# A planned kernel of two graph layers: columns for the attention vectors, reliefs by rows, last stores by halves of rows, and another plan

## The chip, the cores and the metric

The kernel runs on one core of a Trainium2 chip. A core has TensorE (PE: matmuls, each with a load of weights, PEld), VectorE (DVE), ScalarE (ACT), GpSimd (POOL) and SyncE (SP, which here only issues DMAs). Each engine takes its own instructions in order; engines wait for each other by semaphores. The metric is the time of one execution on the device in microseconds (us). Everything is float32.

## The reference

64 graphs of 256 nodes with 256 features, with an adjacency matrix of small integers each, go through two layers. Cut to what matters:

```python
def gat(h, adj, W, a):                       # layer 0, twice: (W1, a1), then (W2, a2)
    Wh = h @ W
    e = leaky_relu(Wh @ a[:256] + swap(Wh @ a[256:]), 0.2)
    att = softmax(where(adj > 0, e, -9e15), axis=1)
    return att @ Wh
h = layernorm(x + gat(gat(x, adj, W1, a1), adj, W2, a2))
x = layernorm(h + relu(h @ w_ff1 + b_ff1) @ w_ff2 + b_ff2)

q, k = x @ Wq + bq, x @ Wk + bk              # layer 1, 8 heads of 32
attn = softmax(q k^T / sqrt(32))
o = sum over r of (attn * (adj == r)) @ (x @ Wv[r] + bv[r])
x = layernorm(x + o @ Wo + bo)
x = layernorm(x + gelu(x @ W1 + b1) @ W2 + b2)
```

## The kernel before

The kernel works on 32 pairs of graphs. One pair goes through `whole_way` (line 1212): `gat_layers` (639), `feed_forward` (stage 0), `attention`, `feed_forward` (stage 2), and two stores (line 1222, 256 KB each). All of a pair's rows lie in a tile `x` of 128 partitions and four blocks of 256 columns: block 2b+j holds the rows 128j to 128j+127 of graph b.

**Matmuls.** A product is written as four strips of 32 weight columns (`by_strips`, line 164), so nearly every matmul of a pair has line 164; in this trace each float32 matmul leaves two records. The products of the feed-forwards and of queries, keys and values are done by a scheme of seven products of blocks in the place of eight: class `Blocks` has the steps `p1` to `p7` (16 records each), with sums of blocks made on DVE before and after; a feed-forward runs two such sets, called a and b, and its second product is `by_seven` (line 887), seven products of 64 records. Attention computes `scores` for a group of four heads, exponentials on ACT (line 1041), mask and half sums on DVE (1045, 1049), then `products` (1063, 1066), `invert` and divide (1075 to 1086), and at the end `into_rows` for each of the two graphs. Four such groups make a pair.

**Layouts.** Rows become columns by a way through DRAM: DVE turns blocks of 32 (line 773), SP stores them (`home`, 778) and gathers them (`yT`, 784, four DMAs). Where that is too slow, at the first and last pairs (`hurried`), PE transposes (`transposed_on_tensor`, line 804).

**The plan.** Which instruction comes next on which engine is decided when the program is built, by a list scheduler in the kernel itself (`run`, line 286). Each pair is a generator; what it yields is a step for PE with the events that it needs, a name that it must hold alone, and buffers. Work for the other engines is handed over by `put` with an assumed cost, a rank and an assumed delay. `run` always takes the earliest thing that can start; among several it goes by `DEGREE` (for PE) or by `RANK` (for the others). `FIRST`, `QKV` and `GROUPS` give the order of the seven products and of the heads, `FLIGHT` the number of pairs under way, `SLACK` how long a step must have been ready, and `CHANGES` (line 32) replaces any of these at given times of the plan's own clock. The resulting order is fixed: the engines take it as it is, however long things last. `START`, `LANDED` and `THERE` (lines 67 to 69) are assumed times at which engines begin and first DMAs land.

**The opening.** Line 173 loads W2 by SP's queue; ACT's queue loads W1 transposed, then a2, broadcast to all partitions (256 KB written), then a1 as columns (2 KB). DVE multiplies W2's rows with a2 and sums them (line 179, four times), which gives the columns W2 a2 beside W2. PE then multiplies W1 with all of it, 256 wide columns and 4 narrow ones per half of W1's rows, and DVE and ACT copy the result to `w12` (lines 188, 189), the weights of the first layer's matmul on xT. Behind these, SP issues every other first load, 13.8 MB in the first 45 us.

**Reliefs.** Layer norm biases and output biases are added to rows once; what they would add wrongly to later products is taken from those products' biases. `relieve` (line 1171) does this for both feed-forwards and for queries and keys: for each block of 128 columns of a weight matrix it makes that block the stationary operand and the bias one moving column, which gives the correction along the partitions:

```python
nc.tensor.matmul(p[:, m:m + 1], lhsT=w[:, ((0, 1), (2, 6))[half][c], rows + at * P:rows + (at + 1) * P],
                 rhs=more[1][:, c:c + 1], start=c == 0, stop=c == KC - 1)
```

One DVE subtraction (line 1181) follows. `relieve_values` does the same for values by rows, with the bias broadcast as stationary operand. `block_sums` and `last_sums` then make the sums of weights that the seven products need.

**Layer norm.** `layernorm` (line 717): ACT squares with a sum (726), POOL takes the root (731, 732), DVE centres and scales (737, 740), each for two blocks of rows. Ahead of it the mean comes either from DVE's addition of rows (`add_rows`, 698) or, after `by_seven`, from ACT (`means`, 712). It takes the blocks of one graph, 2b and 2b+1.

Of the kernel before, what the change touches and what calls it, by code (L numbers as in the profile page):

```python
# [10 lines left out]
F32 = mybir.dt.float32  # L11
# [3 lines left out]
AF = mybir.ActivationFunctionType  # L15
# [15 lines left out]
NORMED = ()  # L31
CHANGES = (
    (27.0, ("rank", "centre", 2),
     ("all", "first", ("a1", "b1", "a2", "a6", "b2", "b6", "a5", "a7", "b7", "b5", "a4", "b4", "a3"))),
    (117.0, ("rank", "piece", 3), ("rank", "halves", -1)),
    (207.0, ("all", "slack", 0.4), ("rank", "exp", -2), ("rank", "scale", 2)),
    (297.0, ("degree", "gat", -1)),
    (387.0, ("degree", "first", -1)),
    (477.0, ("rank", "halves", 2), ("rank", "v", -0.5)),
    (567.0, ("all", "slack", 0.1)),  # L40
    (657.0, ("all", "first", ("a1", "b1", "b2", "a2", "a6", "b6", "a5", "a7", "b7", "b5", "a4", "b4", "a3"))),
    (747.0, ("all", "slack", 0.6), ("rank", "act", -1), ("rank", "turn", 0), ("rank", "divide", 0), ("degree", "fill", 1.5),
     ("rank", "qk", 2)),
    (837.0, ("rank", "mask", -0.5), ("rank", "centre", 2)),
    (927.0, ("rank", "addends", 2)),
    (1017.0, ("rank", "means", -2), ("rank", "sums", -2), ("all", "slack", 0.4)),
    (1197.0, ("rank", "mask", 1)),
    (2187.0, ("rank", "mask", -0.5)),
    (2277.0, ("rank", "exp", -0.5), ("rank", "halves", -0.5)),
    (2457.0, ("rank", "squares", 3)),  # L50
    (2547.0, ("all", "slack", 0.3)),
    (2637.0, ("rank", "normalise", 1.5), ("degree", "first", 2)),
    (2727.0, ("rank", "centre", 1), ("rank", "turn", 1), ("all", "slack", 0)),
    (2817.0, ("all", "slack", 0.2), ("rank", "means", 3)),
# [6 lines left out]
        "normalise": -1, "copies": -2, "seeds": -2, "act": -1, "last": -1, "sums": -0.5, "qk": 1, "v": 1.5, "exp": 3, "mask": 0, "halves": 0, "invert": 3,  # L61
# [5 lines left out]
START = {"tensor": 9.5, "vector": 9.3, "scalar": 9.7, "gpsimd": 0.0, "sync": 36.0}  # L67
LANDED = (("ln0", 15.0), ("ff0", 18.5), ("ff0_last", 26.0), ("ln1", 28.5), ("attention", 34.5), ("ff1", 40.0), ("ff1_last", 43.0))
THERE = ((6.5, 8.0, 13.5), (9.5, 11.0, 27.5), (20.5, 22.0, 35.0))
# [3 lines left out]
def two_layers(ctx: ExitStack, tc: tile.TileContext, t: dict, out: bass.AP, flag: bass.AP):  # L73
# [22 lines left out]
    PART = 64  # L96
# [74 lines left out]
    a2, w1T = passing[:, 0], passing[:, 1].rearrange("p (c m) -> p c m", c=KC)  # L171
    junk = work.tile([P, 2, N], F32, name="h", bufs=HQ)[:, 0]
    nc.sync.dma_start(right[:, :, :D], t["L0_gnn_W2"].rearrange("(c p) m -> p c m", p=P))
    nc.scalar.dma_start(w1T, t["L0_gnn_W1T"].rearrange("(c p) m -> p c m", p=P))
    nc.scalar.dma_start(a2, bass.AP(tensor=t["L0_gnn_a2"].tensor, offset=t["L0_gnn_a2"].offset, ap=[[0, P], [1, 2 * D]]))
    nc.scalar.dma_start(right[:, :, D + 2:], t["L0_gnn_a1c"])
    for s in range(2):
        for c in range(KC):
            nc.vector.scalar_tensor_tensor(
                junk, right[:, c, :D], 1.0, a2[:, s * D:(s + 1) * D], op0=ALU.mult, op1=ALU.mult,  # L180
                accum_out=right[:, c, D + s:D + s + 1])
    both = [bank() for _ in range(KC)]
    for m in range(KC):
        for columns in (slice(0, D), slice(D, D + 4)):
            for c in range(KC):
                by_strips(both[m][:, columns], lhsT=w1T[:, c, m * P:(m + 1) * P], rhs=right[:, c, columns],
                          start=c == 0 and columns.start == 0, stop=c == KC - 1, skip_group_check=True)
    nc.vector.tensor_copy(w12[:, 0], both[0][:, :D + 4])
    nc.scalar.activation(w12[:, 1], both[1][:, :D + 4], AF.Copy)

# [163 lines left out]
    def done_with(name):  # L358
        del alone[name]

# [276 lines left out]
    def gat_layers(pair, to, loads):  # L637
# [37 lines left out]
        for b in range(2):  # L675
# [9 lines left out]
            transposed(to["x"], layernorm(to["x"], ln[0], b, added, biased[0], stage="gat"), normal, b, pair, 0)  # L685
# [19 lines left out]
    def means(y, b, *events):  # L705

        of = {}

        def mean(j):
            if j == 0:  # L710
                of["less"] = small.tile([P, 2], F32, name="less", bufs=8)
            nc.scalar.activation(unread, y[:, 2 * b + j, :], AF.Copy, scale=-1.0 / D, accum_out=of["less"][:, j:j + 1])

        return of, put_each("scalar", 0.45, [lambda j=j: mean(j) for j in range(2)], *events, rank=rank_of["means"])

    def layernorm(r, gb, b, added, *events, stage=None):
# [3 lines left out]
        rows = [r[:, 2 * b + j, :] for j in range(2)]  # L720
# [7 lines left out]
        def root():  # L728
# [4 lines left out]
            if stage in NORMED:  # L733
                nc.gpsimd.tensor_tensor(of["less"], of["less"], rstd, ALU.mult)
# [7 lines left out]
        def normalise(j):  # L742
            nc.scalar.activation(rows[j], rows[j], AF.Identity, bias=of["less"][:, j:j + 1], scale=rstd[:, j:j + 1])

        def onto_all(n, op):
            both = r[:, of_graph(b), :]
            nc.vector.tensor_tensor(both, both, gb[n].rearrange("p (k d) -> p k d", k=1).to_broadcast([P, 2, D]), op)
# [940 lines left out]
```

## Time and profile before

| | us |
|---|---|
| median of 3 runs | 2898.7 |
| lowest and highest | 2896.8, 2900.65 |
| the profiled execution's own time | 2905.58 |
| its span, first to last instruction | 2903.8 |
| PE busy | 2862.7 (99%) |
| DVE busy | 2636.2 (91%) |
| ACT busy | 1908.4 (66%) |
| POOL busy | 284.9 (10%) |

Matmuls are pipelined and their ends are modelled, so a busy PE is not yet a PE at its pace; the pace is read from the records per stage and from the granted clock (1.00 is full). Lines such as `PE ps L164 <- DMA yT<-home: 2.6, 1, 2.6` say: PE, about to write `ps` at line 164, waited for the landing of that DMA, 2.6 us in total, once, 2.6 at most. In a timeline a line gives the start, the length, the engine, the line of the kernel, the operation, what it writes and reads, the number of records, and in brackets the idle time of the engine ahead of it with what ended it. A number such as `128*32` is rows times columns of the stationary operand.

### The profile page before, as it was taken

The numbers are of one execution on the slowest core, as the hardware profiler recorded it, in microseconds if no ns is written. First come the engines' busy times: TensorE is split into PE (matmuls) and PEld (weight loads), VectorE is DVE, ScalarE is ACT, GpSimd is POOL, SyncE is SP. The second block draws the span as 40 slices with busy tenths as digits, with TensorE's granted clock in tenths as the row PEclk, the third lists the DMA queues.
The fourth block names the chain that finished last, engine by engine and source line by source line (L and its number), as shares of the span: only waits on it lengthen the run. The fifth ranks groups of instructions, "written<-read, shape, count | busy, mean of one in ns | idle before, by whom it ended". The sixth has DMA issues, their size and how long they took to land.

```text
span 2903.8 us, 151915 instructions
## 1 busy us (share of the span) xinstructions
PE 2862.7 (99%) x68114; PEld 2021.2 (70%) x68114; DVE 2636.2 (91%) x5873; ACT 1908.4 (66%) x5171; POOL 284.9 (10%) x518
## 2 busy tenths in 40 slices
PE   8999999999999999999999999999999999999997
PEld 5766677676776676676767776766777877767666
DVE  7889998899998999998999999999999999999986
ACT  5656766656766667666677666676666676666765
POOL 0001010101010100001111101101101111010001
PEclk9999999999999999999999999999999999999999
DMA  6222222222222221222222222222222222221100
GB/s 206 75 68 70 69 65 79 72 79 79 65 69 76 83 83 58 78 70 79 79 76 69 69 76 84 74 74 70 72 76 83 76 65 68 83 73 51 54 3 25
DMA packets 207955, 212.11 MB, mean 73 GB/s; under 512 B 22592, under 2 KB 166336, under 8 KB 207040
## 3 DMA queue, kind: packets, MB, share of 16 engines
q1 hardware_dynamic: 206608, 201.79, 21.6%
q8 instruction: 536, 8.78, 1.3%
q14 instruction: 123, 1.01, 0.1%
q10 hardware_dynamic: 688, 0.53, 0.1%
HBM read 137.51 MB, written 64.73 MB: 70 GB/s over the span
## 4 chain that ended last, share of the span: by engine, by line
PE 87%; DVE 6%; DMA 4%; ACT 1%; issue 1%; SPq 1%; ACTq 0%; DVEq 0%; POOL 0%; POOLq 0%
PE ps L164 73%; PE ps L1063 7%; PE ps L1031 4%; PE ps L1066 2%; DMA home<-yb 2%; DVE ff L913 1%; DVE m L1045 1%; DMA yT<-home 1%; SPq L784 1%; DMA rows<-row 1%; DVE x L740 1%; DVE yb L773 1%; DVE h L1049 0%; DVE x L737 0%; DVE x L910 0%
## 5 line engine op out<-in xcount | busy, mean ns | idle before, releaser
L164 PE MATMUL ps<-w_L_gnn_W,ff 128*32 128x128 f32 x14336 | 424.4, 273 | 1.4 <-issue 0.8
L164 PE MATMUL ps<-w_L_gnn_w_ff,ff 128*32 128x128 f32 x14336 | 423.3, 273 | 1.9 <-DVE ff L509 1.1
L164 PEld LDWEIGHTS ps<-w_L_gnn_W,ff 128*32 128x32 f32 x14336 | 393.3, 110 | 41.7 <-issue 19.5
L164 PEld LDWEIGHTS ps<-w_L_gnn_w_ff,ff 128*32 128x32 f32 x14336 | 396.2, 110 | 36.3 <-issue 10.0
L1041 ACT ACTIVATE a<-ps 128x512 f32<-128x512 f32 x512 | 264.3, 601 | 186.5 <-PE ps L1031 180.6
L913 DVE TENSOR_TENSOR ff<-ff 128x1024 f32<-128x1024 f32 x256 | 311.5, 1217 | 55.3 <-PE ps L164 38.9
L731 POOL TENSOR_SCALAR rstd<-squares 128x2 f32<-128x2 f32 x256 | 78.8, 308 | 2591.1 <-ACT unread L726 2590.6
L164 PE MATMUL ps<-yT,w_L_gnn_W1p 128*32 128x256 f32 x5120 | 307.6, 381 | 4.0 <-DMA yT<-home 2.6
L1045 DVE TENSOR_TENSOR m<-a,adj 128x1024 f32<-128x1024 f32 x256 | 307.9, 1215 | 3.7 <-ACT a L1041 3.5
L164 PE MATMUL ps<-yT,w_L_gnn_w_ff1p 128*32 128x256 f32 x5120 | 306.2, 379 | 0.0
L838 ACT ACTIVATE ff<-ps 128x512 f32<-128x512 f32 x384 | 220.9, 587 | 129.6 <-PE ps L164 128.9
L726 ACT ACTIVATE unread<-x,less 128x256 f32<-128x256 f32 x512 | 258.7, 505 | 70.6 <-DVE less L701 54.1
L509 DVE TENSOR_TENSOR ff<-ps,ff 128x512 f32<-128x512 f32 x384 | 255.6, 682 | 38.0 <-PE ps L164 25.2
L1000 ACT ACTIVATE qk<-ps,bqk 128x256 f32<-128x256 f32 x256 | 109.6, 470 | 222.6 <-PE ps L164 222.3
L164 PE MATMUL ps<-xw,e 128*32 128x256 f32 (+1 forms) x4032 | 245.0, 383 | 1.3 <-ACT xw L631 1.3
L164 PEld LDWEIGHTS ps<-yT,w_L_gnn_W1p 128*32 128x32 f32 x5120 | 165.3, 110 | 109.3 <-ACT ff L838 7.5
L164 PEld LDWEIGHTS ps<-yT,w_L_gnn_w_ff1p 128*32 128x32 f32 x5120 | 168.2, 110 | 99.9 <-ACT ff L838 0.5
L737 DVE SCALAR_TENSOR_TENSOR x<-x,less,b_ln 128x256 f32<-128x256 f32 x512 | 227.4, 477 | 7.3 <-ACT unread L726 6.2
L740 DVE SCALAR_TENSOR_TENSOR x<-x,rstd,b_ln 128x256 f32<-128x256 f32 x512 | 229.1, 477 | 1.3 <-POOL rstd L732 1.3
L910 DVE TENSOR_TENSOR x<-ps,x 128x256 f32<-128x256 f32 (+1 forms) x384 | 193.7, 505 | 21.9 <-PE ps L164 17.3
L732 POOL TENSOR_TENSOR rstd<-rstd,mhalf 128x2 f32<-128x2 f32 x256 | 205.5, 803 | 21.3
L164 PEld LDWEIGHTS ps<-xw,e 128*32 128x32 f32 x4032 | 135.7, 111 | 84.1 <-issue 2.6
(141 smaller groups left out, 4992.7 us busy)
## 6 DMA issues: line engine op xcount, KB each, us to landing
home<-yb SPq DMA_DIRECT2D x182, 256.0 KB, 2.2
yT<-home SPq DMA_DIRECT2D x728, 64.0 KB, 2.1
rows<-row SPq DMA_DIRECT2D x60, 512.0 KB, 4.0
x<-in_x SPq DMA_DIRECT2D x32, 512.0 KB, 3.9
out<-x SPq DMA_DIRECT2D x64, 256.0 KB, 2.5
input<-in_xT SPq DMA_DIRECT2D x30, 512.0 KB, 4.1
input<-in_adjT SPq DMA_DIRECT2D x29, 512.0 KB, 4.2
m<-in_adjT SPq DMA_DIRECT2D x3, 512.0 KB, 8.6
```

What stands on the lines that cost most here:

```text
L164: nc.tensor.matmul(to[at:at + DH], lhsT=lhsT[:, at:at + DH], rhs=rhs, **flags)
L509: nc.vector.tensor_tensor(self.target(*where), self.bank["z"], self.target(*where), ALU.add)
L726: nc.scalar.activation(unread, rows[j], AF.Square, bias=of["less"][:, j:j + 1], accum_out=squares[:, j:j + 1])
L732: nc.gpsimd.tensor_tensor(rstd, rstd, mhalf[:, :2], ALU.pow)
L737: nc.vector.scalar_tensor_tensor(rows[j], rows[j], of["less"][:, j:j + 1], g, op0=ALU.add, op1=ALU.mult)
L740: nc.vector.scalar_tensor_tensor(rows[j], rows[j], rstd[:, j:j + 1], beta, op0=ALU.mult, op1=ALU.add)
L838: return put("scalar", 0.5, lambda: nc.scalar.activation(target(c, h), of, AF.Copy), event, rank=rank_of["copies"])
L910: return put("vector", us, lambda: nc.vector.tensor_tensor(to, of, to, ALU.add), *events, rank=rank_of["last"], frees=frees)
L913: return put("vector", 1.14, lambda: nc.vector.tensor_tensor(to, a, b, op), *events, rank=rank_of["sums"])
L1041: nc.scalar.activation(a[n][q][:, k], ps[2 * q + k], AF.Exp)
L1045: nc.vector.tensor_tensor(m[n][q], a[n][q], adj, ALU.mult)
L1063: nc.tensor.matmul(po[o * DH:(o + 1) * DH, :N], lhsT=v[:, b, jc, at:at + DH], rhs=e[o // 2][:, o % 2, jc * N:(jc + 1) * N], start=r == jc ...
```

## The change

Five things change at once; lines are those of the new kernel where not said otherwise.

1. **First weights.** The broadcast of a2 and the DVE reductions go. W2 is also loaded transposed (256 KB, ACT's queue, in the place of a2), and a2 and a1 come as columns in one array (4 KB, SP's queue, second). PE makes the wide columns first, then W2 a2 from the transposed W2, then all four narrow columns with W1.
2. **Reliefs.** `relieve` makes the bias, broadcast over 32 columns, the stationary operand, and the weights the moving one, 128 (feed-forwards) or 64 columns (queries and keys together) per matmul; DVE turns the result by blocks of 32 and subtracts.
3. **Last stores.** For the last pair's last layer norm, `means` and `layernorm` take the blocks j and 2+j (one half of the rows of both graphs) in the place of the two blocks of one graph, and the two last stores go by these halves.
4. **The plan.** `CHANGES` is another table, and `START`, `LANDED` and `THERE` have other numbers; the assumed costs of the new reliefs are 0.22 per block and 0.65 for DVE. The order of nearly all instructions differs. Per pair the matmuls are the same.
5. **Without effect on the program:** an unused way of the layer norm (`NORMED`) goes; a local name in `by_eight`, which no stage uses, is changed.

The diff, cut to its core:

```diff
-    (27.0, ("rank", "centre", 2),
-     ("all", "first", ("a1", "b1", "a2", "a6", "b2", "b6", "a5", "a7", "b7", "b5", "a4", "b4", "a3"))),
...
+    (27.0, ("degree", "gat", 0.5), ("rank", "squares", 3)),
+    (117.0, ("rank", "exp", 0.5), ("rank", "ratios", 0),
+     ("all", "qkv", ("a1", "b1", "a2", "b2", "a6", "a5", "b6", "a7", "a4", "b5", "b7", "a3", "b4", "s0", "s1", "b3")),
+     ("degree", "rows", 0.5), ("rank", "centre", 2), ("rank", "seeds", 1.5)),
...
-START = {"tensor": 9.5, "vector": 9.3, "scalar": 9.7, "gpsimd": 0.0, "sync": 36.0}
-LANDED = (("ln0", 15.0), ("ff0", 18.5), ("ff0_last", 26.0), ("ln1", 28.5), ("attention", 34.5), ("ff1", 40.0), ("ff1_last", 43.0))
-THERE = ((6.5, 8.0, 13.5), (9.5, 11.0, 27.5), (20.5, 22.0, 35.0))
+START = {"tensor": 9.8, "vector": 9.7, "scalar": 9.7, "gpsimd": 0.0, "sync": 36.5}
+LANDED = (("ln0", 17.4), ("ff0", 20.2), ("ff0_last", 25.5), ("ln1", 28.3), ("attention", 32.9), ("ff1", 40.5), ("ff1_last", 43.6))
+THERE = ((8.2, 10.7, 14.9), (12.0, 13.5, 26.8), (21.4, 22.9, 34.3))
...
-    nc.scalar.dma_start(a2, bass.AP(tensor=t["L0_gnn_a2"].tensor, offset=t["L0_gnn_a2"].offset, ap=[[0, P], [1, 2 * D]]))
-    nc.scalar.dma_start(right[:, :, D + 2:], t["L0_gnn_a1c"])
-    for s in range(2):
+    nc.sync.dma_start(right[:, :, D:], t["L0_gnn_ac"])
+    nc.scalar.dma_start(w2T, t["L0_gnn_W2T"].rearrange("(c p) m -> p c m", p=P))
...
-            nc.vector.scalar_tensor_tensor(
-                junk, right[:, c, :D], 1.0, a2[:, s * D:(s + 1) * D], op0=ALU.mult, op1=ALU.mult,
-                accum_out=right[:, c, D + s:D + s + 1])
...
+    wide(0)
+    nc.vector.tensor_copy(w12[:, 0, :D], both[0][:, :D])
+    wide(1)
+    nc.scalar.activation(w12[:, 1, :D], both[1][:, :D], AF.Copy)
+    narrow_columns(thin[0], w2T, slice(D, D + 2))
+    nc.vector.tensor_copy(right[:, :, D:D + 2], thin[0][:, :, :2])
+    narrow_columns(thin[1], w1T, slice(D, D + 4))
+    nc.vector.tensor_copy(w12[:, :, D:], thin[1])
...
+        if last_of_all(pair, stage):
+            normal["added"] = [means(y, by_halves(j), d24, d7, *([d3] * j)) for j in range(2)]
+        else:
+            normal["added"] = [means(y, pair_of(g), d24, d7, d3) for g in range(2)]
...
-        for m in range(of):
-            half, at = divmod(m, of // 2)
+        for h in range(2):
             for c in range(KC):
-                nc.tensor.matmul(p[:, m:m + 1], lhsT=w[:, ((0, 1), (2, 6))[half][c], rows + at * P:rows + (at + 1) * P],
-                                 rhs=more[1][:, c:c + 1], start=c == 0, stop=c == KC - 1)
-        return put("vector", 0.15, lambda: nc.vector.tensor_tensor(bias, bias, p[:, :of], ALU.subtract),
-                   took(of * 0.4), frees=["bank"])
+                for q in range(HQ):
+                    nc.tensor.matmul(p[q * DH:(q + 1) * DH, h * per * DH:(h + 1) * per * DH],
+                                     lhsT=more[1][:, c:c + 1].to_broadcast([P, DH]),
+                                     rhs=w[:, ((0, 1), (2, 6))[h][c]].rearrange("p (a q j) -> p q a j", q=HQ, j=DH)[:, q],
+                                     start=c == 0, stop=c == KC - 1)
+        turned = p[:, 256:256 + 2 * per * DH]
+
+        def subtract():
+            nc.vector.transpose(turned, p[:, :2 * per * DH])
+            nc.vector.tensor_tensor(bias, bias, turned.rearrange("p (h a i) -> p h a i", h=2, i=DH)[:, :, :, 0], ALU.subtract)
+
+        return put("vector", 0.65, subtract, took(0.22 * per), frees=["bank"])
...
+        def store(b):
+            if last_of_all(pair, 2):
+                nc.sync.dma_start(out[2 * pair:2 * pair + 2, b * P:(b + 1) * P].rearrange("g p d -> p g d"),
+                                  to["x"].rearrange("p (g j) d -> p j g d", j=2)[:, b])
+            else:
+                nc.sync.dma_start(out[2 * pair + b].rearrange("(c p) d -> p c d", p=P), to["x"][:, of_graph(b), :])
```

## The prediction

> **What bounds the kernel now.** I read the busy times first, then stages of equal work, then what TensorE (PE) waited for, then the timeline of each place found.
>
> ```profile
> span 2903.8 us, 151915 instructions
> PE 2862.7 (99%) x68114; PEld 2021.2 (70%) x68114; DVE 2636.2 (91%) x5873; ACT 1908.4 (66%) x5171; POOL 284.9 (10%) x518
> ```
>
> PE is busy for all but 41.1 us. Whether a busy PE is also at its pace is told by stages (us; busy time and records of PE, PEld, DVE, ACT, POOL; granted clock; DMA share; GB/s):
>
> ```profile
> 25.00:30.00 5.00, 5.00 (x50) 3.21 (x52) 4.68 (x13) 3.30 (x9) 0.00 (x0) 0.66 0.81 276
> 45.00:50.00 5.00, 5.00 (x52) 3.18 (x55) 2.38 (x8) 1.35 (x3) 0.00 (x0) 0.66 0.39 111
> 280.00:300.00 20.00, 15.80 (x268) 9.34 (x264) 12.15 (x25) 8.44 (x19) 0.00 (x0) 0.91 0.48 143
> 1488.00:1576.00 88.00, 88.00 (x2116) 61.55 (x2112) 81.67 (x183) 59.31 (x162) 9.08 (x16) 1.00 0.24 75
> 2800.00:2850.00 50.00, 46.50 (x1096) 31.44 (x1088) 41.90 (x83) 29.56 (x76) 2.62 (x6) 0.97 0.04 14
> 2850.00:2904.00 54.00, 41.92 (x1254) 35.49 (x1246) 33.08 (x62) 24.30 (x70) 5.75 (x11) 0.93 0.08 24
> ```
>
> In the middle one pair of graphs takes 88 us and PE is busy throughout, at full clock: nothing is to be had there but matmuls, and the change removes none of a pair's. What a change can move lies in the opening, in scattered waits up to 400 us, in the last 200 us, and in stretches at 0.66 of the clock. PE's waits in total, times, longest:
>
> ```profile
> PE ps L164 <- DMA xw<-in_L_gnn_a1c: 3.8, 1, 3.8
> PE ps L1063 <- ACT a L1041: 3.5, 2, 3.1
> PE ps L164 <- DVE ff L509: 2.7, 6, 1.1
> PE ps L164 <- DMA yT<-home: 2.6, 1, 2.6
> ```
>
> The change hits the first directly; the others belong to the order of the work, which the new plan rewrites.
>
> **First weights.** Now: a2's broadcast lands at 7.78 (DVE's first L179), four DVE reductions end at 9.62, the column a1c lands at 10.26, and the first matmul on xT starts at 12.38. After: W2T (256 KB like the broadcast, same place in ACT's queue) should land at about 7.8; two narrow products of 32 records (24 such weight loads took 0.45, so 0.6 each) and two small copies with their handoffs (0.4 each, from 0.17 for a copy of 128x2) follow: 7.8 + 0.6 + 0.4 + 0.6 + 0.4 = 9.8, **2.6 earlier**. If the column array, now second on SP, lands as late as a1c did, it is 0.2. SP issues everything behind it about 0.46 later (one issue); xT landed at 7.8 and has 1.5 to spare.
>
> **Reliefs.** L1179's 32 records took 3.66 twice (22.27 is 3.47 on the chain, 42.50 to 46.16) and 16 took 1.87. The new form has 32 records of 32 weight columns: 64 of the form 128x128 with 32 take 1.75, so 0.87; for queries and keys, 64 wide, 0.44 to 0.87, taken as 0.66. PE is relieved of 2.79 + 1.21 + 2.79 = **6.8**. DVE gets three transposes (0.45 for 128x256 from PSUM, twice, and about 0.3), +1.2.
>
> Both times L1179 is followed by half speed: 64 records of xw,e take 4.80 (from 27.11) and 5.35 (from 46.16) where 3.47 is the pace. The page counts L1179 as busy, yet the clock fell to 0.66. [...]
>
> **What takes that gain.** By the rows so far PE would be 9.4 ahead, plus 1.3 of clock in the first relief. But the path leaves PE:
>
> ```profile
> 41.38 0.91 ACT L631 ACTIVATE xw<-xw,rs 128x256 f32<-128x256 f32 x2 [1.47 <-DVE rs L627]
> 44.50 1.06 ACT L386 ACTIVATE adj<-input 128x1024 uint8<-128x1024 int32 x1 [2.21 <-DMA input<-in_adjT]
> 45.46 0.89 ACT L631 ACTIVATE xw<-xw,rs 128x256 f32<-128x256 f32 x2
> ...
> 46.16 5.35 PE L164 MATMUL ps<-xw,e 128*32 128x256 f32 x64
> ```
>
> The fourth pair's adjacency lands at 44.5, the end of a queue of 13 MB at 1.0 DMA share; the change moves no bytes out of it. Today the conversion stands between the two pairs of scales (L631) of the first pair's second layer. In the new built order it stands ahead of both, and DVE's last weights for the second scale stand behind the sum x,less of the first half. PE ends the last relief at about 40.9 (its weights land at 40.0). Then: conversion 44.5 to 45.5, first scale to 46.4, first half of xw,e at half clock (after an idle 5.5; the idle 5 before 291.72 also cost clock) to 49.9, sum 1.0, weights 1.0, squares and scale to 53.2, second half to 54.9, one transpose (0.87) 55.8, third pair's xT (3.5) 59.3, xw,e 61.0, a wait of 0.8 for the layer norm, transpose 62.7, xw,e 64.4. Today the same work and 1.73 more is done at 64.39. So the opening comes out **+1.8**, not -10. Bounds: -8.2 if the landing is early enough not to matter, +3.5 if DVE's extra 1.2 and one scale come on top.
>
> **The order behind it.** I counted, in the built order of both, the PE work between a producer and its consumer, with rows as prices (a product of 16 records 0.865; 64 records of the last weights 1.745; scores 1.05; attention products 2.17). It says where a wait can be, and today's trace says how much work a handoff needs:
>
> - From attention's last rows to the feed-forward's first product, through DRAM: needs 20.5 (pair 1: 271.17 to 291.72, with 15.8 of work in it); 19.3 elsewhere had no wait. New: 23.4 for pair 1, but 17.5 for pair 0. That takes away 2.6 and 1.7 of clock, and 1.0 of two waits beside it, and adds 2.4: **-2.9** (-5.3 to -1.5).
> - Scores to products: 7.9 passed where PE waited (pair 31: 2826.49 to 2834.40, with 4.1 of work), 6.5 of work was once enough; 7.2 taken. Pair 31 now has 7.6 or more: 3.5 of waiting and 1.7 of clock go, **-5.2** (nothing to gain only if a table load of 1.28 lands in it).
> - Other waits at both ends, 3.65 in all (0.66, 0.98, 0.14, 0.20, 0.44, 0.12, 1.11), lose their places. New short ones: scores with 5.4, 6.3, 6.7 and 6.5 of work (pairs 2, 3, 30, 30) at 7.2 make 3.9; three times the sixth product stands right behind the first, where today a like handoff with none between (pair 2's p4) waited 0.96: 2.9. **+3.2** (-3.6 to +6).
> - The middle, 400 to 2300, waited 0.9 + 3.2 + 2.1 = 6.2. New distances there are larger where it waited (p1 to p2 3.5 for 1.7, values to products 6.1 for 2.6), smaller at one (4.4 to 2.6, p4 to the seven products). I take two thirds, **-4** (-6.2 to 0).
>
> **Last stores by halves.** Only rows 1 and 3 wait for the last product now. But from 2891.26 ACT does four means (0.54 apart) and four squares (0.64) nearly without a break to 2896.48; in the new order the same eight stand in it, and both stores still carry 256 KB. **0**, at best -0.4, which is the one gap of 0.37.
>
> **Sum.** 1.8 - 2.9 - 5.2 + 3.2 - 4 = -7.1. The profiled execution took 2905.58, of which 2903.8 is span; the runs' median is 2898.7. The difference carried to the median gives **2891.6** (-0.24%).
>
> **Rivals.**
> 1. *The opening keeps its gain*: the landing does not decide, -8.2 in place of +1.8: 2881.6. For it: GB/s falls to 276 in 25 to 30, so the queue has slack that an earlier start may use. Against: 10 us from issue to landing.
> 2. *The new short handoffs wait in full*, and the middle keeps its waits: -7.1 + 2.4 + 4 is 2898. This is no change.
> 3. *Slower: the attention's second rows.* In 18 middle pairs the new order leaves 4.3 of PE work between the last products and into_rows of b=1 (today 18.3). DVE must in that time invert, then add the first half's rows, which wait for PE (1.74 + 0.25 + 0.35), then divide (0.42): 2.9. Pairs 3 and 31 have 4.3 today and passed without a wait (425.90 to 430.04). It decides once two more DVE operations of 1.22 stand in it, 5.3 for 4.3; DVE is 93% busy there. Price 18 x 1.0: 2891.6 + 18 = 2909.6.
>
> **Chances.** The forecast with the part of its spread beyond 0.2% (about what a measurement of this kernel tells from no change, 5.8 us): 0.34; rival 1, 0.20; rival 2 and the forecast's slower edge within 0.2%, 0.28; rival 3 and other new waits of that size, 0.18. So faster 0.54, same 0.28, slower 0.18. The range goes from below rival 1 (opening -8.2, middle -6.2, no new wait for pair 0) at 2876 to 2906, short of rival 3's full price.
>
> **What would show it.** The first matmul on xT near 9.8; L1180's 32 records in about 0.9; PE idle some 5 us before xw,e at 46.4, with ACT waiting for in_adjT; no wait over 1 us near 290 for pair 1 and none at pair 31's scores; 88 us a pair in the middle at 1.00 clock. I am wrong in the opening if xw,e of the first pair's second layer starts before 44, in the middle if into_rows is what PE waits for there, and in the order if new waits at the ends pass 10 us.

## The result and the profile after

The changed kernel is slower: median 2916.82 us (2915.64 to 2922.12) beside 2898.97 us (2896.80 to 2900.65) of the kernel before, six runs each; ratio 1.0063, interval 1.0053 to 1.0074. The forecast was 2891.6 and the range ended at 2906.

The profiled execution of the changed kernel took 2915.64 (span 2913.9), 1.2 below its median; that of before took 2905.58, 6.6 above its own. So the two profiles differ by 10.1 where the medians differ by 17.9: the profiles show where time goes, the ratios how much. The granted clock is not the difference: between the first and the last matmul the changed kernel's profile has 10.2 us at half clock, that of before 13.7.

Page of the changed kernel: span, then busy time, share and records of each engine.

```profile
span 2913.9 us, 151945 instructions
PE 2858.0 (98%) x68162; PEld 2000.0 (69%) x68162; DVE 2632.2 (90%) x5869; ACT 1887.3 (65%) x5157; POOL 286.1 (10%) x518
```

PE is busy for 4.7 less than before, and stands still for 55.9 instead of 41.1. The stages tell where (us; PE, PEld, DVE, ACT, POOL with records; granted clock; DMA share; GB/s). First the changed kernel:

```profile
0.00:100.00 100.00, 80.36 (x1687) 52.98 (x1691) 73.40 (x219) 52.10 (x143) 5.52 (x15) 0.95 0.50 167
...
400.00:900.00 500.00, 490.25 (x11757) 343.85 (x11760) 452.68 (x1014) 319.06 (x896) 56.57 (x86) 1.00 0.23 73
900.00:2700.00 1800.00, 1796.33 (x42940) 1259.82 (x42936) 1661.78 (x3700) 1194.04 (x3248) 174.41 (x326) 1.00 0.23 74
```

Then the kernel before, for the stage where they part:

```profile
400.00:900.00 500.00, 499.19 (x12014) 351.44 (x12009) 463.61 (x1031) 331.60 (x913) 46.98 (x90) 1.00 0.24 75
```

From 400 to 900 PE now stands still for 9.7 where it stood 0.8, and does 257 records less. Behind 900 a pair takes its 88 us as before (88.2 on average from pair 8 to pair 28), at a granted clock of 1.00 from 900 to 2700 in both profiles. What PE waits for there (in total, times, longest):

```profile
PE ps L167 <- DVE x L909: 6.9, 4, 2.6
PE ps L167 <- DVE ff L912: 2.4, 5, 1.7
```

Both are steps of the feed-forward's second product. One of the four places, DVE and PE in order of start:

```profile
649.57 0.87 DVE L751 SCALAR_TENSOR_TENSOR x<-x,rstd,b_ln 128x256 f32<-128x256 f32 x2
653.30 0.43 DVE L470 TENSOR_TENSOR sums_yT<-yT 128x256 f32<-128x256 f32 x1 [2.87 <-DMA yT<-home]
653.64 0.70 DVE L772 STREAM_TRANSPOSE yb<-x 128x512 f32<-128x512 f32 x1
...
655.26 0.42 DVE L909 TENSOR_TENSOR x<-ps,x 128x256 f32<-128x256 f32 x1
```

```profile
649.49 3.68 PE L167 MATMUL ps<-w_L_gnn_w_ff,ff 128*32 128x128 f32 x128
655.73 1.52 PE L167 MATMUL ps<-w_L_gnn_w_ff,ff 128*32 128x128 f32 x48 [2.56 <-DVE x L909]
```

DVE is free at 650.4 and takes its next instruction, a sum on columns that come by way of DRAM. It stands there for 2.87 until they land. PE's next product needs DVE's addition L909, which stands behind that sum and 2.0 of other work: it starts at 655.26, and PE has stood since 653.17. No instruction of DVE or PE is slow here; two of DVE's are in the wrong order. The same picture returns once a pair in pairs 5 to 8 (PE idle 1.2 at 474.40, 1.9 at 564.72, 2.6 at 655.73, 1.3 at 745.44).

Why the columns are late: the turned rows have one buffer `yb`, so the second half's turn waits for the first half's store. DVE's groups at the turn, before and then after (busy, mean ns | idle just before them):

```profile
L773 DVE STREAM_TRANSPOSE yb<-x 128x512 f32<-128x512 f32 x182 | 128.0, 704 | 2.0 <-DMA home<-yb 1.3
```

```profile
L772 DVE STREAM_TRANSPOSE yb<-x 128x512 f32<-128x512 f32 x182 | 128.1, 704 | 58.4 <-DMA home<-yb 58.3
```

The same 182 turns, the same 704 ns; but in the old order the store had landed nearly every time, and in the new one DVE stands 58.3 us ahead of 42 of them, all over the span. (A *stand* is a time in which an engine is idle because its next instruction cannot start.) Not all of this is lost: where DVE stands 58.3 over the span, PE stands 9.7 from 400 to 900 and 3.7 from 900 to 2700. It costs where PE's next product is queued behind it, as in the 6.9 for the addition above. For the pair above the first turn is at 636.56; its store, issued 0.46 behind the load of an adjacency matrix (637.63, 512 KB), took 4.7 to land (the median of the 182 stores is 2.7 here, 2.2 in the kernel before); the second turn came at 642.85, its gather was issued at 648.87 and landed at 653.2.

### The profile page after: what moved, and what is told of

Its sections match the earlier page's. It is cut to its first block, busy times and chain, and to the rows that moved or that the text cites. A ratio compares the mean times of both kernels' runs of the same rounds, so it can differ in the third digit from the quotient of the medians.

```text
span 2913.9 us, 151945 instructions
## 1 busy us (share of the span) xinstructions
PE 2858.0 (98%) x68162; PEld 2000.0 (69%) x68162; DVE 2632.2 (90%) x5869; ACT 1887.3 (65%) x5157; POOL 286.1 (10%) x518
## 4 chain that ended last, share of the span: by engine, by line
PE 85%; DVE 7%; DMA 6%; issue 1%; ACT 1%; SPq 1%; DVEq 0%; POOL 0%; POOLq 0%; ACTq 0%
PE ps L167 71%; PE ps L1065 7%; PE ps L1033 4%; DMA home<-yb 3%; PE ps L1068 2%; DVE ff L912 1%; DVE yb L772 1%; DVE x L751 1%; DVE x L748 1%; DMA yT<-home 1%; DVE x L711 1%; DVE x L909 0%; SPq L783 0%; DVE qk L522 0%; DVE v L1008 0%
## 5 line engine op out<-in xcount | busy, mean ns | idle before, releaser
L167 PE MATMUL ps<-w_L_gnn_w_ff,ff 128*32 128x128 f32 x14336 | 416.7, 273 | 12.5 <-DVE x L909 6.9
L744 POOL TENSOR_SCALAR rstd<-squares 128x2 f32<-128x2 f32 x256 | 84.8, 331 | 2600.6 <-ACT unread L739 2598.6
L167 PE MATMUL ps<-yT,w_L_gnn_w_ff1p 128*32 128x256 f32 x5120 | 315.0, 379 | 0.0
L909 DVE TENSOR_TENSOR x<-ps,x 128x256 f32<-128x256 f32 (+1 forms) x384 | 192.9, 502 | 25.0 <-PE ps L167 20.9
L843 ACT ACTIVATE ff<-ff,c_L_gnn_b_ff 128x256 f32<-128x256 f32 x384 | 175.3, 502 | 61.1 <-DVE ff L522 60.5
```

Source lines behind the costliest of these rows:

```text
L167: nc.tensor.matmul(to[at:at + DH], lhsT=lhsT[:, at:at + DH], rhs=rhs, **flags)
L909: return put("vector", us, lambda: nc.vector.tensor_tensor(to, of, to, ALU.add), *events, rank=rank_of["last"], frees=frees)
```

## The experiments

Theory **order**: the new order of instructions costs the time, at the places above. Rival **edits**: the new first weights, reliefs and stores cost it (more DVE work and more waiting in the opening). Each ratio is to the kernel before, run beside it.

### The two halves of the change

`edits_old_order`: all edits, but the table and constants of before and the old assumed costs of the reliefs; PE's built order is that of before.

```diff
-START = {"tensor": 9.8, "vector": 9.7, "scalar": 9.7, "gpsimd": 0.0, "sync": 36.5}
+START = {"tensor": 9.5, "vector": 9.3, "scalar": 9.7, "gpsimd": 0.0, "sync": 36.0}
...
-        return put("vector", 0.65, subtract, took(0.22 * per), frees=["bank"])
+        return put("vector", 0.15 * (1 if per > 2 else 2), subtract, took(0.8 * per), frees=["bank"])
```

> The new first weights, reliefs and last stores, but with the tables and the assumed costs of the kernel before, so that PE's order of steps is the old one. Theory 'order': the lost time lies in the new order of the work, and the edits by themselves give what was priced (2.6 us for the first weights, 6.8 for the reliefs, some clock), less what the fourth pair's adjacency, landing at 44.3 to 44.5, holds back; in the old order only the second half of the first pair's second layer stands behind it. So 5 to 9 us below the kernel before: 2890 to 2894. Rival 'edits': one of the edits costs time by itself (the transposes on DVE, the banks, the clock); then 2905 or more.

2902.61, ratio 1.0008 (0.9999 to 1.0017). The edits neither cost nor gain, so neither expectation held. PE is busy for 11.2 less, and stands still in the first 100 us for 16.9 instead of 11.7: its wait for the column a1c (3.8) is gone, and its waits for ACT's scales are 7.7 instead of 1.3, of which 4.0 stand behind the late adjacency.

`new_order_old_edits`: the edits of before, with the new table, constants and assumed costs.

```diff
-        return put("vector", 0.15, lambda: nc.vector.tensor_tensor(bias, bias, p[:, :of], ALU.subtract),
-                   took(of * 0.4), frees=["bank"])
+        return put("vector", 0.65 if of > 2 else 0.325, lambda: nc.vector.tensor_tensor(bias, bias, p[:, :of], ALU.subtract),
+                   took(of * 0.11), frees=["bank"])
```

> The first weights, reliefs and last stores of the kernel before, with the tables and assumed costs of the changed kernel, so that PE's order of steps is the new one. Theory 'order': the opening waits for the adjacency anyway, so the old edits cost it little (0 to 3 us), and the middle and end lose what the changed kernel loses: 2913 to 2921. Rival 'edits': 2897 to 2901, as before.

2925.44, ratio 1.0092 (1.0076 to 1.0107), above the expected range. The order alone costs 26 with the old first weights, reliefs and stores; with the new ones it costs 16 by the ratios (1.0063 less 1.0008 of 2899). The rival falls: in the new order the edits save 8, in the old one nothing.

The edits one by one in the kernel before (its order kept): `first_weights_only` takes part 1 of the change, `reliefs_only` part 2. The diff of the first:

```diff
-    nc.scalar.dma_start(right[:, :, D + 2:], t["L0_gnn_a1c"])
+    nc.sync.dma_start(right[:, :, D:], t["L0_gnn_ac"])
+    nc.scalar.dma_start(w2T, t["L0_gnn_W2T"].rearrange("(c p) m -> p c m", p=P))
...
```

> The kernel before with the new first weights alone, its order unchanged. Theory: the first matmul on xT starts 2.5 earlier, and this is lost at the landing of weights and adjacency before 100 us, as nearly all of the edits' gain was in the old order: within 2 us of the kernel before. Rival: it comes through: 2.5 us below.

2900.93, ratio 1.0006 (0.9997 to 1.0016). The diff of the second:

```diff
-                nc.tensor.matmul(p[:, m:m + 1], lhsT=w[:, ((0, 1), (2, 6))[half][c], rows + at * P:rows + (at + 1) * P],
-                                 rhs=more[1][:, c:c + 1], start=c == 0, stop=c == KC - 1)
+                                     lhsT=more[1][:, c:c + 1].to_broadcast([P, DH]),
+                                     rhs=w[:, ((0, 1), (2, 6))[h][c]].rearrange("p (a q j) -> p q a j", q=HQ, j=DH)[:, q],
...
```

> The kernel before with the new reliefs alone, its order unchanged. Theory: PE's 6.8 us of relief turn into waiting for landings (the fourth pair's adjacency at 44.5), and 0 to 3 us come through. Rival: they cost, because DVE's transposes hold up its additions at a time when PE waits for DVE: 2 to 5 us above the kernel before.

2898.59, ratio 0.9994 (0.9985 to 1.0003). Each is nothing that this measurement can tell.

### Which stand

DVE stands at two kinds of places: at the turn, for the store of the one buffer, and at the sums, for the columns that come by way of DRAM. ACT has a third, in the opening: the conversion of the fourth pair's adjacency. Each is first taken out alone.

`sums_behind`: in the changed kernel the twelve sums (line 470) of pairs 5 to 8 that stand ahead of a waited addition are emitted behind DVE's next addition of the second product.

```diff
+HELD = (684, 686, 688, 821, 823, 825, 958, 960, 962, 1095, 1097, 1099)
...
-                piece["emit"]()
+                if engine == "vector" and ordinal[0] - 1 in HELD:
+                    held.append(piece["emit"])
+                else:
+                    piece["emit"]()
+                    if engine == "vector" and "by_seven" in name and "add" in name:
+                        while held:
+                            held.pop(0)()
```

> The changed kernel, with one thing moved: for pairs 5 to 8, in four places, DVE's three sums of blocks that wait for the way through DRAM stand behind the addition that releases PE's sixth product of the second feed-forward matrix, and not ahead of it. Theory 'order': PE's waits of 1.2, 1.9, 2.6 and 1.3 us there (and some of the 1.7 at 839) go: 4 to 7 us less than the changed kernel, 2910 to 2913. Rival: the sums are then late for the product that reads them, and PE waits there for as long: 2916 to 2918.

2915.87, ratio 1.0054 (1.0040 to 1.0068), which the changed kernel's interval overlaps: about 3 by the ratios, perhaps nothing, where the theory had 4 to 7. PE's idle time from 400 to 900 fell from 9.7 to 6.1, and that behind 900 rose from 3.7 to 7.4.

`conversion_late`: the fourth pair's conversion on ACT and the load behind it are held until PE's 17th step, behind the scales of the first pair.

```diff
+        small_adj.pair = largest.pair = xT.pair = pair
...
+                if getattr(piece["emit"], "pair", None) == 3:
+                    held.append(piece["emit"])
```

> The changed kernel, with one thing moved: ACT's conversion and DVE's maximum of the fourth pair's adjacency (and the load that reuses its buffer) stand behind the scales of the first pair's second layer. Theory: PE's idle 5.1 us ahead of 45.8 and the half clock behind it (1.7) go: 5 to 8 us less than the changed kernel, 2909 to 2912. Rival: the fourth pair's adjacency or the third pair's columns are then late, and PE waits there instead: 2916 to 2918.

2916.76, ratio 1.0064 (1.0051 to 1.0078): nothing, where the theory had 5 to 8. In its profile the last product of pair 2 ends at 418.9 instead of 424.7, that of pair 28 at 2728.7 instead of 2731.5. A lead of 5.8 won in the opening is half gone there.

`two_turned`: a second buffer for the turned rows, with the built order unchanged.

```diff
-            blocks = work.tile([P, 8, 2, 32], F32, name="yb")
+            blocks = work.tile([P, 8, 2, 32], F32, name="yb", bufs=2)
```

> The changed kernel with a second buffer for the rows turned by DVE on their way to DRAM; the built order is the same. In the changed kernel DVE stands 58.3 us in all at this turn, waiting for the store of the half before it (2.0 in the kernel before), and the way of the second half through DRAM starts that much later. Theory 'late handoff' (the new order puts the second half's turn right behind the first's, so that its columns land late, and DVE's sums and PE stand for them): the 58 us of standing go, each second half lands 1 to 2 us earlier, and PE's idle time in 400 to 900 falls from 9.7 to 4 to 7; 3 to 8 us in all, 2909 to 2914. Rival: DVE stands somewhere else for as long and PE's waits stay: 2916 to 2918.

2916.63, ratio 1.0050 (1.0037 to 1.0063): 4 by the ratios, again with intervals that overlap, though the stand at the turn is gone. DVE's group there, and then what DVE waits for from 400 to 900:

```profile
L772 DVE STREAM_TRANSPOSE yb<-x 128x512 f32<-128x512 f32 x182 | 128.0, 703 | 0.7
```

```profile
DVE sums_yT L470 <- DMA yT<-home: 17.4, 5, 4.9
```

In the changed kernel that last wait was 8.2:

```profile
DVE sums_yT L470 <- DMA yT<-home: 8.2, 4, 2.9
```

DVE gets to the sums earlier and stands there instead, as the rival said; PE's idle time in the stage is 11.8. One stand had covered the other in part.

### The stands together

`two_moves` joins `sums_behind` and `two_turned`; `three_moves` adds `conversion_late`.

```diff
+HELD = (684, 686, 688, 821, 823, 825, 958, 960, 962, 1095, 1097, 1099)
...
-            blocks = work.tile([P, 8, 2, 32], F32, name="yb")
+            blocks = work.tile([P, 8, 2, 32], F32, name="yb", bufs=2)
```

> The changed kernel with the second buffer for turned rows and with DVE's sums behind the addition in pairs 5 to 8, but with the conversion of the fourth pair's adjacency where it was. Theory 'DVE stands': these two belong together (the first alone only moves the standing from the turn to the sums, 58 us there for 10 more here, the second alone leaves the late handoff), so most of the 9 us of the three moves comes from them: 2908 to 2912. Rival 'opening': the conversion made the difference, and the two give nothing: 2915 to 2918.

2907.38, ratio 1.0038 (1.0024 to 1.0052).

```diff
+        small_adj.pair = largest.pair = xT.pair = pair
```

> The changed kernel with three things at once: the second buffer for turned rows, DVE's sums behind the addition in pairs 5 to 8, and the fourth pair's conversion behind the first pair's scales. Theory 'waits add up': 5 for the opening, 3.6 in 400 to 900 and 3 to 5 for the turns come through once the handoffs are no longer late: 2903 to 2909. Rival 'what one place gives, the next takes': 2914 to 2918, as with each move alone.

2907.83, ratio 1.0025 (1.0014 to 1.0036). Of the changed kernel's 0.63% the first leaves 0.38 and the second 0.25.

`sums_behind_combine` is `three_moves` with the sums one step later, behind the next combination (line 912 of the changed kernel) instead of the next addition; the diff is to `three_moves`.

```diff
-                    if engine == "vector" and "by_seven" in name and "add" in name:
+                    if engine == "vector" and "by_seven" in name and "combine" in name:
```

> The three moves, with the sums of pairs 5 to 8 one step later again, behind the sum of two blocks that releases PE's third product (the one that waits 6.6 us in all for it in the run with three moves). Theory 'DVE stands': PE's waits of 0.8 to 1.7 us there go, 2 to 4 us less than the three moves: 2904 to 2906. Rival: the sums are late for the first product that reads them: 2907 to 2910.

2897.53, ratio 0.9995 (0.9986 to 1.0004), better than both expectations: **the whole loss is gone**, with PE's order and all edits those of the changed kernel. Its stages, and what PE waits for from 400 to 900:

```profile
400.00:900.00 500.00, 497.60 (x11868) 349.41 (x11864) 460.10 (x1031) 318.86 (x900) 59.06 (x90) 1.00 0.24 73
900.00:2700.00 1800.00, 1798.02 (x43156) 1271.88 (x43152) 1673.64 (x3698) 1201.56 (x3269) 174.56 (x326) 1.00 0.24 74
```

```profile
PE ps L169 <- DVE ff L931: 1.7, 1, 1.7
PE ps L169 <- DVE x L928: 0.6, 1, 0.6
```

The waits for the addition (here L928) have shrunk from 6.9 to 0.6.

Which of the three does it? `sums_far` is the changed kernel with the sums behind the combination alone; `sums_far_two_turned` adds the second buffer.

```diff
+                    if engine == "vector" and "by_seven" in name and "combine" in name:
+                        while held:
+                            held.pop(0)()
```

> The changed kernel with only the twelve sums of pairs 5 to 8 moved, behind the sum of two blocks that releases PE's third product. One buffer for turned rows, the conversion where it was. Theory 'standing at the sums': the 7 to 9 us of PE's idle time in 400 to 900 go by this alone: 2907 to 2911. Rival 'late handoff': without the second buffer the turn takes over the standing, and little goes: 2913 to 2917.

2915.46, ratio 1.0046 (1.0034 to 1.0058): the rival held. From 400 to 900 PE stands still for 2.3, as wanted, but for 7.6 from 900 to 2700, while DVE still stands at the turn:

```profile
L782 DVE STREAM_TRANSPOSE yb<-x 128x512 f32<-128x512 f32 x182 | 128.6, 707 | 59.7 <-DMA home<-yb 59.3
```

```diff
-            blocks = work.tile([P, 8, 2, 32], F32, name="yb")
+            blocks = work.tile([P, 8, 2, 32], F32, name="yb", bufs=2)
```

> The same with the second buffer for turned rows, the conversion where it was. Theory: the buffer adds the small waits behind 900 (4 to 6 us by the run with the buffer alone) to what the sums give, and the opening's 3 to 5 us stay lost: 2900 to 2904. Rival: the opening was worth nothing here either: 2896 to 2899.

2903.24, ratio 1.0006 (0.9997 to 1.0014). The stand at the turn is gone here:

```profile
L782 DVE STREAM_TRANSPOSE yb<-x 128x512 f32<-128x512 f32 x182 | 128.6, 706 | 0.8
```

Against the changed kernel, by the ratios: the buffer alone gives 4, the sums alone 5, and neither interval is clear of the changed kernel's; both give 16.5 (1.0063 to 1.0006), 12 of them by the buffer once the sums are out of the way (2915.46 to 2903.24, measured side by side). The late conversion on top gives 3 (1.0006 to 0.9995, intervals that overlap).

The last products of three pairs show how a lead is kept or lost (us, one profile each; PE's built order is the same in all five):

| last product ends | pair 2 | pair 8 | pair 28 |
|---|---|---|---|
| changed kernel | 424.7 | 966.7 | 2731.5 |
| two_turned | 425.9 | 974.2 | 2733.3 |
| sums_far | 426.1 | 962.5 | 2731.7 |
| sums_far_two_turned | 425.7 | 960.7 | 2720.7 |
| sums_behind_combine | 419.0 | 955.0 | 2713.0 |

`sums_far` leads the changed kernel by 4.2 at pair 8 and by nothing at pair 28: what PE wins, it loses again while DVE stands at the turn. With the buffer it leads by 6.0 and then 10.8.

### The table and its state

Could the plan be mended by changing one of its settings? `mask_rank_kept` leaves one rank of the new table out; `new_then_old` takes the new table up to 297 and that of before from 387 on.

```diff
-     ("rank", "piece", -0.5), ("rank", "turn", -1), ("all", "flight", 7), ("rank", "mask", 2)),
+     ("rank", "piece", -0.5), ("rank", "turn", -1), ("all", "flight", 7)),
```

> The changed kernel without one setting of its new table: at 387 the rank of the masks stays 0 and does not become 2. The built order is the changed kernel's up to there; behind it DVE no longer has the three sums that wait for the way through DRAM ahead of the addition that releases the sixth product, in pairs 5 to 8. Theory 'order' (the time is lost between 400 and 900, by DVE standing there): the idle time of PE in 400 to 900 falls from 9.7 to 2 to 4 us, and the whole is 4 to 8 us below the changed kernel, 2909 to 2913. Rival (what is won in one stretch is waited for in the next, as in the run with the sums moved): 2915 to 2918.

3060.35, ratio 1.0553 (1.0538 to 1.0567). The expectation failed: from 400 to 900 PE's idle time falls a little (7.2), but over the span it waits 37.1 for DVE's masks and 24.7 for ACT's scales.

```diff
-    (387.0, ("rank", "seeds", 1),
...
+    (387.0, ("degree", "first", -1)),
+    (477.0, ("rank", "halves", 2), ("rank", "v", -0.5)),
...
```

> The changed kernel with its new table up to 297, and from 387 on the table of the kernel before. Theory 'order, middle': the opening and the stretch to 400 lose what the changed kernel loses there (3 to 6 us against the old order with the new edits, 2902.6), and the rest runs like the kernel before: 2904 to 2909. Rival 'order, all of it': the settings only suit the state that they were set for, so the old table from another start is no better than the new one: 2914 or more.

3121.65, ratio 1.0768 (1.0753 to 1.0782): PE waits 53.3 for columns by way of DRAM. Both are far slower than either whole table, so neither says where the 18 us went.

### The kernel before, once more, and a better version

`before_again` is the kernel before, unchanged, for one more profile; it has no edit.

> The kernel before, unchanged, for a second profile: the first one came from an execution 6.7 us above the median. Theory: some of the waits that the prediction took for the old order's own (3.2 us in 900 to 1400 and 1.9 in 1900 to 2300) are accidents of that execution, since the same order of steps with the new edits has 0.5 and 1.0 there; then a second profile, near the median of 2899, shows under 3 us of them in all, and the middle had nothing to give. Rival: they belong to the order; then they stand here too, 5 to 6 us.

2903.89 once, span 2902.1. PE's idle time from 900 to 2300 is 4.1 here, 5.4 in the first profile of the same kernel and 1.7 in that of `edits_old_order`: between the two expectations, and inconclusive.

`edits_old_order_conv` is `edits_old_order` with the late conversion (until PE's 16th step).

```diff
+HELD_TO = 16
...
+                if getattr(piece["emit"], "pair", None) == 3:
+                    held.append(piece["emit"])
```

> The new edits in the old order, and ACT's conversion and DVE's maximum of the fourth pair's adjacency stand behind all scales of the first pair's second layer. Theory: in the old order the edits' gain of 9.4 is held back by that landing (the wait for the scale there is 4.0 us, and the gain at 130 us is only 1.6); with the conversion out of the way 3 to 6 us come through: 2896 to 2900. Rival: the next load holds PE back in its place: 2901 to 2904.

2900.35, ratio 0.9997 (0.9985 to 1.0008): 3 below `edits_old_order` by the ratios, with intervals that overlap.

`old_order_end` adds to `edits_old_order_conv` one setting for the last pairs, which gives pair 31's scores more work before their products (from 4.1 and 4.8 to 7.6 and 6.5 us of PE work).

```diff
-    (2727.0, ("rank", "centre", 1), ("rank", "turn", 1), ("all", "slack", 0)),
+    (2727.0, ("rank", "centre", 1), ("rank", "turn", 1), ("all", "slack", 0), ("degree", "attention", -2)),
```

> The new edits in the old order with the conversion late, and one setting more, from 2727 on: attention's steps are taken first. In the built order the last pair's scores then have 7.6 and 6.5 us of PE's work between them and their products in the place of 4.1 and 4.8. Theory: PE's wait of 3.5 us at the last pair and its half clock (1.7) go, and no other opens: 3 to 5 us less than without it, so 0.1 to 0.2% below the kernel before: 2895 to 2897. Rival: the wait moves to the attention's second rows or to the transposes, which have 11 us in the place of 18: 2899 to 2901.

2895.88, ratio 0.9989 (0.9980 to 0.9998): the only version whose interval lies below the kernel before, by 0.1%. The old order with the new edits, the late conversion and a better end is the best that these runs have.

## Why the prediction was wrong

To set parts of two orders beside each other I take for a pair the end of its last product less the PE work that stands ahead of it in the built order, at the prediction's prices (the opening's first weights and reliefs not counted as such work). How much this excess differs between the two profiles gives the terms:

| part | predicted | changed − before |
|---|---|---|
| opening, to pair 0 | +1.8 | +1.7 |
| handoffs at the start, pair 0 to 2 | −2.9 and part of +3.2 | +2.5 |
| the middle, pair 2 to 28 | −4 | **+10.3** |
| pair 28 to 31 | −5.2 and part of +3.2 | −2.7 |
| behind the last product | 0 | −1.7 |
| sum | −7.1 | +10.1 |

The other 7.8 between the medians these two profiles cannot place.

**First weights and opening: right.** The first matmul on xT starts at 9.88 (predicted 9.8), the relief's 32 records take 1.08 (about 0.9), and the late landing eats the gain in the way described. The agreement of +1.7 with +1.8 is partly luck: where the prediction's sum ends, PE is done at 63.3 and not at 64.4, which makes +0.6, and the rest comes later. ACT and PE of the changed kernel:

```profile
44.28 1.06 ACT L399 ACTIVATE adj<-input 128x1024 uint8<-128x1024 int32 x1 [7.21 <-DMA input<-in_adjT]
...
45.79 3.64 PE L167 MATMUL ps<-xw,e 128*32 128x256 f32 x32 [5.10 <-ACT xw L644]
```

ACT stands 7.21 for the adjacency, and PE 5.10 for the scale behind it (predicted 5.5, until 46.4). The 1.3 of clock that the prediction saw behind the first relief did not come here: the first 64 records on xw,e take 5.11, and 4.80 in the kernel before. Half clock now begins at 22.4, in PE's wait of 2.71 ahead of them.

**The end: right in kind.** Pair 31's wait for its scores is gone, with 2.7 left of the 5.2 beside new short waits. The halves of rows give 0, as predicted: `edits_old_order` has the same stores and 11.9 behind its last product, as before; the changed kernel's 10.2 comes with its order.

**The start: half right.** PE's wait of 2.6 for pair 1's columns is gone. But PE's waits from 250 to 400 are now:

```profile
PE ps L167 <- DVE v L1008: 3.4, 2, 2.6
PE ps L167 <- DVE sums_yT L470: 2.8, 1, 2.8
```

**The middle: the step that failed.** "New distances there are larger where it waited ... I take two thirds, -4". The distances were counted as PE work between a producer and its consumer. That is the right measure only if the engine between them is free when its turn comes. DVE takes its instructions in the built order (in the pair above the addition stood behind a sum that stood 2.87), it is 90% busy, and in the new order it stands 58.3 at the turn and 8.2 at the sums of pairs 5 to 8, ahead of additions for which PE waits. None of it shows in PE's distances, but DVE's and SP's built order would have shown where it threatens: the sums stand ahead of the additions, and in the pair above the second turn was due 4.6 behind the first (641.12 and 636.56), while its buffer's store was issued 1.5 behind the first. That this store takes 4.7 is in the trace alone. The prediction's -4 for the middle was +10.3; nine of the ten lost us fall between pairs 2 and 8 (+9.3).

**Rival 3** had a price nearest to the result, 2909.6, by another mechanism: `into_rows` is in no place of the middle what PE waits for. So the slower side was near in size (18 over the forecast, where 25 were measured) and wrong in cause.

**Where the expected gain went:** with the edits alone PE is busy for 11.2 less in the profile, and 5.2 of it comes back as waiting in the opening. The rest one profile of each does not tell, since that of the edits is 3 below its median and that of before 6.6 above; the medians leave nothing. Shown by experiment: the order holds the loss; without the two stands on DVE 16.5 of the 18 are gone, and with the late conversion besides, all of it, within the intervals. Behind pair 8 it is not the clock: it is 1.00 from 900 to 2700 in all five profiles of the table. There the buffer brings `sums_far_two_turned` 9.2 ahead of `sums_far` (from 1.8 at pair 8 to 11.0 at pair 28), of which PE's idle time shows 5.5 (7.6 less 2.1). Not settled: where the rest lies in time that is shown as busy; executions of one kernel differ by about as much (25 of the kernel before: 2895.90 to 2906.66).

## What to carry to other kernels

When a plan is changed, count distances on every in-order engine, not on the one that bounds: an instruction that can stand for a DMA must not be queued ahead of what the bounding engine waits for, and a buffer with one copy turns the next turn into such an instruction. Take two stands out together before you call either harmless, since one covers the other: here 4 and 5 us alone, neither clear of nothing, were 16.5 together. A table of settings hangs together: leaving one of them out made this kernel 5% slower, which tells nothing of what that setting was worth.

## What the runs showed of the hardware

Between the first and the last matmul the profile of the kernel before has four stretches of half clock of 3.4 us each (from 26.0, 46.5, 292.2 and 2835.2), that of the changed kernel one of 3.4 (from 22.4) and one of 6.8 (from 42.9). A stand of PE ahead of one product was followed by it in one profile and not in another. `two_turned`, PE idle for 1.68 us ahead of a product at 843.48 (columns as in the stages above):

```profile
841.00:844.00 3.00, 1.32 (x40) 0.81 (x28) 2.96 (x7) 2.97 (x8) 1.71 (x2) 0.99 0.23 66
844.00:847.40 3.40, 3.40 (x67) 2.96 (x60) 3.10 (x10) 0.98 (x3) 0.25 (x1) 0.50 0.09 24
```

The changed kernel, the same 1.68 us ahead of the same product at 838.97:

```profile
836.00:839.00 3.00, 1.32 (x34) 0.64 (x26) 2.93 (x9) 2.59 (x8) 1.27 (x1) 1.00 0.22 74
839.00:842.40 3.40, 3.40 (x104) 2.72 (x112) 3.33 (x10) 1.49 (x5) 0.69 (x1) 1.00 0.20 57
```

Once 3.4 us at 0.50 followed, 67 records where the other did 104; once the clock stayed at 1.00. From 80 us to the last matmul, the profiles of the kernel before and of the changed one have together eight stands of PE of 0.96 to 1.32 us, and half clock followed none of them within 3.4 us. Of the seven longer ones it followed two, both in the kernel before (2.58 ahead of 291.72, 3.05 ahead of 2834.40), and none of the five in the changed kernel (1.68, 1.86, 2.56, 2.59, 2.78). Such a stretch costs PE up to 1.7 us, an estimate from 3.4 us at 0.50. So a stand of 1.68 to 3.05 us cost here itself, or itself and up to 1.7. The times of one kernel differ together with the clock: of the 25 executions of the kernel before that ran beside `two_turned`, the 15 with a mean clock of 0.996 average 2901.8 and the 8 with 0.997 average 2898.4.

Half clock also came where PE did not stand. In the kernel before, the old reliefs' 32 records with a single moving column take 3.63 (from 22.11) and 3.73 (from 42.50); PE is shown as busy for all of 22.3 to 26.0 and of 42.5 to 46.4, and half clock sets in at 26.0 and 46.5, 0.3 behind their ends. The two sets of 64 records on xw,e behind them take 4.80 and 5.35, where 64 of them at a clock of 1.00 take 3.66 (from 77.39). So the prediction read its rows rightly. The new form did not end it: in the changed kernel its 32 records take 1.08 (from 18.05) and 1.37 (from 39.32, with two records of another product among them), and half clock sets in at 22.4 and 42.9, now in PE's waits of 2.71 and 5.10; in `reliefs_only` the clock is 0.93 from 0 to 50 and 0.93 from 50 to 100, where the kernel before has 0.93 and 1.00.
